# Moving weight loads, statistics, degrees and one scaling within the last attention batch of a graph-attention and aggregation kernel

## The chip, the cores and the metric

The kernel runs on one core of a Trainium2 chip. The metric is the device time of one execution in microseconds (us), as a median of several runs. A core has five engines with an instruction stream each: TensorE (PE) for matrix products, VectorE (DVE), ScalarE (ACT), GpSimd (POOL) and SyncE (SP); SP here does nothing but issue DMA transfers. The engines run side by side and wait for each other with semaphores. Within one engine the instructions run in the order in which they were written.

## The reference

Input `x` has 16 batches of 1024 nodes with 256 channels; `adj` is a 1024 x 1024 matrix. Layer 0, cut to what matters:

```python
g   = relu(einsum('bcn,bnm->bcm', x^T, adj * A_s) * para)   # A_s from the nodes' means
q   = g^T in 4 heads;  k, v = (x @ kv_w) in 4 heads
out = softmax(q k^T * scale) v
x1  = layernorm(x + out)
```

Layer 1 uses the same matrix, normalised by degrees:

```python
A_norm = A + eye(n)
deg    = A_norm.sum(0) + A_norm.sum(1) - diagonal(A_norm)
dinv   = rsqrt(deg)
agg    = einsum('nm,bmd->bnd', A_norm * dinv[:, None] * dinv[None, :], x1)
h      = relu(batchnorm(agg @ W1.T + b1))
y      = layernorm(x1 + batchnorm(h @ W2.T + b2))
```

The batch norms take their statistics over all batches and nodes, so layer 1 has stages that can't begin before the one ahead of them has gone through all batches.

## The kernel before

**Stages.** A first stage goes through the 16 batches and does layer 0 for each. It overlaps the preparation of batch b+1 (weights `wg`, products `p1` to `p7`) with the attention of batch b. A second stage aggregates and does the first linear layer, a third the second linear layer, a fourth the last norm and the output. The change lies in the last attention batch (b = 15), where there is no batch 16 to prepare; layer 1 is prepared in its place.

**Attention.** The work of one batch is 32 units `(b, pr, qh, m)`: a pair of heads, a half of the queries, and a block of 128 keys. `scores(i)` (L1058) has PE write a PSUM tile `ps` and ACT take its exponential into `p` (a pool of four buffers). `outputs(i)` (L1074) has PE add `p` times the values into two PSUM tiles `po`, and DVE add `p` into `acc`, the sums of the softmax. Eight units make a group with one `po` pair and one `acc`. At its end ACT copies one `po` into `oT`, DVE adds the other (L1105), transposes it into `oS` (L1115), and SP writes it out and gathers it back by rows. After both groups of a pair of heads, `normalise` (L1127) has PE sum `acc` over the partitions (`den`, L1134); the sums travel by way of DRAM into columns `dcol`, and `residual` (L1152) takes reciprocals on DVE (`r_all`) and has POOL scale and add (L1161, L1162).

**The order.** PE, ACT, DVE and SP follow the order in which the program issues. The units are taken two at a time, in 16 bursts u = 0 to 15 per batch. In a burst the program issues the scores of its two units, then `back(j - 1)`, the outputs of the two before, and then what hangs on the burst. For the last batch that is the table `last`, keyed by u; `before_last` is the same for batch 14. A place under 16 in the lists of `(function, places)` is a burst of batch 14, a place from 16 on is burst place - 16 of batch 15. Entries of one burst run in the order in which they were put into the table. So each line of these tables fixes where a piece of work stands in the queue of every engine that it uses.

**Preparation of layer 1.** For the transposed adjacency, SP loads it as squares of 32 x 32 (`load_adjacency_squares`, L1244: four transfers of 128 KB in pieces of 128 B, alternating between two single buffers, those of `xS` and `crow`); DVE transposes within the squares (`transpose_adjacency`, L1251); ACT sums a block's columns (`adjacency_columns`, L1255). `degrees` (L1260) has three small DVE instructions and a power on POOL. `row_of_degrees` (L1267) transposes the result on DVE and has SP write it to DRAM and read it back as a row on all partitions. `add_identity` (L1272) is on POOL, `scale_adjacency(m)` (L1277) on DVE. `load_weights` (L1199) loads W1 and W2, 512 KB each, and `transpose_weights` (L1206) turns them on PE and copies them on ACT. `load_x1l` (L1293) loads a batch of x1, 1 MB. `statistics_x1` (L1175) computes the layer norm's statistics of batch 14, two blocks per call, on DVE and ends in a chain of four small POOL instructions; `finish_x1` (L1180) applies it on ACT and stores x1.

**The end of attention.** After the last burst, `outputs` of the last unit issues `scale_adjacency(2)` and then the last `acc` addition (L1108 to L1110). Then `aggregate_first(m)` (L1299) runs the first batch's aggregation on PE for m = 0 to 7, with the scalings 3 to 7 issued at m = 0, the last `den` (`den_last`) after m = 1, and the sums `aT` for the next aggregations on DVE beside it. Each m needs its scaled block; the PSUM tiles of m = 0 are those that the last `po` held.

Of the kernel before, what the change touches and what calls it, by code (L numbers as in the profile page):

```python
# [515 lines left out]
def fast_path(  # L516
# [20 lines left out]
    B, N, C = x.shape  # L537
# [28 lines left out]
    def tile_o(name):  # L566
        return psum["o"].tile([P, HALF], F32, tag="o", name=name)
# [167 lines left out]
    with (  # L735
# [338 lines left out]
        def outputs(i):  # L1074
            b, pr, qh, m = units[i]
            s, p = st[b], A.pop(i)
            if m == 0:
                G[b, pr, qh] = {
                    "po": [tile_o(f"po_{i}_{kh}") for kh in range(2)],
                    "acc": accp.tile([P, N], F32, tag="acc", name=f"acc_{i}"),  # L1080
                }
            g = G[b, pr, qh]
            for hd in range(2):
                h = 2 * pr + hd
                for kh in range(2):
                    r = slice(kh * D, (kh + 1) * D)
                    nc.tensor.matmul(  # L1087
                        g["po"][kh][hd * D : (hd + 1) * D, :], s["v"][r, m, h * D : (h + 1) * D],
                        p[r, hd * HALF : (hd + 1) * HALF], start=(m == 0), stop=(m == NCH - 1),
                    )  # L1090
            def sums():
                if m == 0:
                    g["p0"] = p
                elif m == 1:
                    nc.vector.tensor_add(g["acc"], g.pop("p0"), p)
                else:
                    nc.vector.tensor_add(g["acc"], g["acc"], p)  # L1097

            if i < len(units) - 1:
                sums()  # L1100
            if m == NCH - 1:
                k = (b * PAIRS + pr) * 2 + qh
                g["oT"] = op.tile([P, HALF], F32, tag="oT", name=f"oT_{k}")
                nc.scalar.copy(g["oT"], g["po"][0])
                nc.vector.tensor_add(g["oT"], g["po"][1], g["oT"])  # L1105
                if (b, pr) != (B - 1, PAIRS - 1):
                    squares(b, pr, qh)
            if i == len(units) - 1:  # L1108
                scale_adjacency(2)
                sums()  # L1110

        def squares(b, pr, qh):
            k = (b * PAIRS + pr) * 2 + qh
            oS = osp.tile([P, HALF], F32, tag="oS", name=f"oS_{k}")
            nc.vector.transpose(oS, G[b, pr, qh]["oT"])  # L1115
            nc.sync.dma_start(o_d[k].rearrange("q i j d -> (q i) (j d)"), oS)
            rows_of.append((squares_to_rows, (b, pr, qh)))
# [159 lines left out]
        def scale_adjacency(m):  # L1277
            nc.vector.scalar_tensor_tensor(
                aht[m], aht[m], dinv[:, m : m + 1], aht["row"], op0=ALU.mult, op1=ALU.mult
            )  # L1280
# [43 lines left out]
        with tc.manual_schedule(  # L1324
# [27 lines left out]
            def back(j):  # L1352

                for i in bursts[j]:
                    outputs(i)
                b, pr, qh, m = units[bursts[j][-1]]
                if m == NCH - 1 and qh == 1:
                    sums.append((normalise, (b, pr)))
                    for q in range(2):
                        full.append((residual, (b, pr, q)))  # L1360
                    if pr == PAIRS - 1:
                        for f in (statistics_x1, finish_x1):
                            for ns in (range(NCH // 2), range(NCH // 2, NCH)):
                                late.append((f, (b, ns)))

            last, before_last = {}, {}
            for u, todo in (
                (1, (load_weights,)), (6, (load_x1l, 0)), (8, (degrees,)), (9, (row_of_degrees,)),
                (10, (transpose_weights, 0)), (11, (transpose_weights, 1)),
                (12, (add_identity,)), (13, (scale_adjacency, 0)), (14, (scale_adjacency, 1)),  # L1370
            ):
                last.setdefault(u, []).append((todo[0], todo[1:]))
            for f, places in (
                (transpose_adjacency, (9, 11, 13, 15, 17, 19, 21, 23)),
                (load_adjacency_squares, (6, 9, 9, 11, 13, 15, 17, 19)),
                (adjacency_columns, (11, 13, 14, 16, 18, 20, 22, 23)),
            ):
                for m, u in enumerate(places):
                    where = before_last if u < PERB else last
                    where.setdefault(u % PERB, []).append((f, (m,)))  # L1380
            for u, n in ((9, 6), (10, 7)):
                before_last.setdefault(u, []).append((adjacency_rows, (n,)))
            for i in range(4):
                ns = range(2 * i, 2 * i + 2)
                last.setdefault(6 + i, []).append((statistics_x1, (B - 2, ns)))
            for u, ns in ((13, range(2)), (14, range(2, 5)), (15, range(5, NCH))):
                last.setdefault(u, []).append((finish_x1, (B - 2, ns)))
            last[15].append((load_x1l, (1,)))
# [319 lines left out]
    with tc.tile_pool(name="hl", bufs=4) as hl, tc.tile_pool(name="o2p", bufs=1) as o2p:  # L1708
# [89 lines left out]
        for b in range(B):  # L1798
# [59 lines left out]
            for c in range(CC):  # L1858
                last = b == B - 1 and c == CC - 1
# [160 lines left out]
def kernel(tc: tile.TileContext, *args):  # L2020


    with tc.tile_pool(name="flag", bufs=1, space=DRAM) as flag:
        good_d = flag.tile([1, 1], I32, name="good_d")
        fast_path(tc, *args, good_d)
        good = tc.nc.values_load(good_d[0:1, 0:1], min_val=0, max_val=2 * P)
        with tc.If(good < 2 * P):
            general_path(tc, *args)
# [30 lines left out]
```

## Time and profile before

| what | value |
|---|---|
| median of 3 runs | 2470.86 us (2469.76 to 2471.12) |
| the profiled execution | 2469.28 us |
| its span, first to last instruction | 2467.5 us |
| PE busy | 2425.2 us |
| DVE busy | 1840.3 us |
| ACT busy | 1231.6 us |
| POOL busy | 479.9 us |

Stretches of the last attention batch, 20 us each, busy time in us:

| from, to | PE | DVE | ACT | POOL | DMA GB/s |
|---|---|---|---|---|---|
| 1500, 1520 | 20.00 | 16.69 | 15.44 | 4.19 | 96 |
| 1520, 1540 | 18.64 | 17.26 | 12.78 | 8.56 | 178 |
| 1540, 1560 | 18.66 | 14.17 | 12.71 | 7.03 | 61 |
| 1560, 1580 | 18.47 | 19.69 | 9.86 | 15.31 | 106 |
| 1580, 1600 | 20.00 | 19.46 | 0.93 | 8.77 | 1 |

Positions in time are us from the start of the span. Durations and spacings come from one profiled execution. A busy PE is a PE with matmuls in its pipeline: the next one begins before the one ahead has ended, so spacings of starts say more than sums of durations.

### The profile page before, as it was taken

To read this page: it belongs to the slowest core of one execution; us is meant where nothing else is said; L and a number is where in the kernel's file an instruction comes from. 1 tells how busy PE (TensorE), PEld (TensorE's weight loads), DVE (VectorE), ACT (ScalarE), POOL (GpSimd) and SP (SyncE) were. 2 spreads that over 40 slices of the span, in tenths; PEclk is the share of its full clock that TensorE was granted. 3 is DMA by queue.
4 is the path that set the end of the run, shared out by engine and by line. 5 is a ranking of instruction groups with operands and counts; after the bars stand their busy time and mean duration, and the time that the engine had idled before them with its cause. 6 is when DMAs were issued, how large, how long until landed. Compare 5 with 4: busy or idle time off the path is not lost.

```text
span 2467.5 us, 32796 instructions
## 1 busy us (share of the span) xinstructions
PE 2425.2 (98%) x12462; PEld 1035.2 (42%) x12462; DVE 1840.3 (75%) x2528; ACT 1231.6 (50%) x1535; POOL 479.9 (19%) x487
## 2 busy tenths in 40 slices
PE   8999999999999999999999999999999999999997
PEld 4343443443434434434434343344444444434455
DVE  5678878878888888788788888856555555578568
ACT  6375665765765766757657667311010010144458
POOL 0021112211211211121112113522112212000026
PEclk9999999999999999999999999999999999999999
DMA  3123232332232231323322327222122122255559
GB/s 136 31 48 84 54 53 69 69 51 67 39 82 60 41 86 54 52 69 69 53 68 47 72 52 116 54 101 102 69 86 102 68 85 102 91 200 175 182 190 340
DMA packets 414647, 220.42 MB, mean 89 GB/s; under 512 B 353168, under 2 KB 386448, under 8 KB 406032
## 3 DMA queue, kind: packets, MB, share of 16 engines
q1 hardware_dynamic: 409120, 167.36, 27.6%
q0 software_dynamic: 4832, 50.34, 4.9%
q8 instruction: 100, 1.64, 0.3%
q14 instruction: 67, 0.55, 0.1%
q10 hardware_dynamic: 528, 0.52, 0.1%
HBM read 134.49 MB, written 83.69 MB: 88 GB/s over the span
## 4 chain that ended last, share of the span: by engine, by line
PE 83%; DVE 10%; ACT 3%; DMA 2%; issue 1%; SPq 0%; POOL 0%; DVEq 0%; POOLq 0%
PE ps L1066 17%; PE po L1087 17%; PE pgb L896 7%; PE b_agg L1564 4%; PE pga L896 4%; PE c_agg L1564 4%; PE pk L993 3%; PE po L1846 3%; PE pv L1006 2%; PE a_agg L1564 2%; PE b_h L1596 2%; PE b_o L1772 2%; PE pgc L896 2%; PE pgd L896 2%; PE c_h L1596 2%; PE c_o L1772 1%
## 5 line engine op out<-in xcount | busy, mean ns | idle before, releaser
L1071 ACT ACTIVATE p<-ps 128x1024 f32<-128x1024 f32 x512 | 497.4, 1021 | 182.2 <-PE ps L1066 123.2
L1097 DVE TENSOR_TENSOR acc<-acc,p 128x1024 f32<-128x1024 f32 x384 | 501.4, 1306 | 52.3 <-ACT p L1071 28.9
L1066 PE MATMUL ps<-qT,kT 64*64 64x512 f32 x4096 | 488.3, 592 | 0.3 <-ACT p L1071 0.3
L1087 PE MATMUL po<-p,v 64*64 64x512 f32 x4096 | 485.6, 589 | 0.0
L1161 POOL TENSOR_TENSOR o<-o,r_all 128x512 f32<-128x512 f32 x62 | 95.9, 1555 | 1104.8 <-DVE r_all L1155 989.9
L1087 PEld LDWEIGHTS po<-p,v 64*64 64x64 f32 x4096 | 159.4, 133 | 280.1 <-issue 273.2
L1066 PEld LDWEIGHTS ps<-qT,kT 64*64 64x64 f32 x4096 | 152.4, 133 | 285.9 <-issue 248.5
L847 DVE SCALAR_TENSOR_TENSOR wg<-wg,adj_s 128x1024 f32<-128x1024 f32 x128 | 149.7, 1217 | 24.6 <-ACT wg L843 24.6
L838 ACT ACTIVATE wg<-crow,ccol 128x1024 f32<-128x1024 f32 x128 | 146.7, 1146 | 6.1 <-PE pg L978 6.1
L843 ACT ACTIVATE wg<-wg 128x1024 f32<-128x1024 f32 x128 | 135.9, 1062 | 0.9
L993 PE MATMUL pk<-xT,kvw_s 128*128 128x512 f32 x256 | 121.9, 598 | 3.1 <-ACT drow L1140 3.1
L1006 PE MATMUL pv<-kvw_s,xT 128*128 128x256 f32 x512 | 123.9, 385 | 0.0
L1006 PEld LDWEIGHTS pv<-kvw_s,xT 128*128 128x128 f32 x512 | 95.0, 190 | 50.3 <-issue 13.6
L906 ACT ACTIVATE qT<-qT 128x512 f32<-128x512 f32 x60 | 37.1, 626 | 149.8 <-DVE qT L909 145.3
L896 PE MATMUL pgb<-wg,S 128*128 128x512 f32 x240 | 111.0, 605 | 0.0
L896 PE MATMUL pga<-wg,x 128*128 128x512 f32 x240 | 109.6, 599 | 0.7 <-ACT qT L919 0.7
L1564 PE MATMUL a_agg<-ahT,x1l 128*128 128x512 f32 x240 | 108.1, 593 | 0.7 <-ACT agg L1312 0.7
L1564 PE MATMUL b_agg<-aT,x1S 128*128 128x512 f32 x240 | 107.9, 592 | 0.0
L1162 POOL TENSOR_TENSOR x<-x,o 128x512 f32<-128x512 f32 x62 | 106.9, 1734 | 2.4
L656 ACT COPY p_agg<-a_agg 128x512 f32<-128x512 f32 x15 | 8.8, 586 | 183.3 <-PE a_agg L1564 179.5
L1675 ACT ACTIVATE hl<-hl,bn_sh,bn_sg 128x1024 f32<-128x1024 f32 x64 | 75.6, 1232 | 40.7 <-DMA hl<-h 38.1
L692 POOL TENSOR_TENSOR x1S<-x1l 128x512 f32<-128x512 f32 x15 | 19.4, 1293 | 352.9 <-PE c_agg L1564 350.1
(234 smaller groups left out, 3495.8 us busy)
## 6 DMA issues: line engine op xcount, KB each, us to landing
h<-hw POOLq DMA_DIRECT2D x16, 2048.0 KB, 6.6
hl<-h SPq DMA_DIRECT2D x32, 1024.0 KB
x<-x POOLq DMA_DIRECT2D x16, 1024.0 KB, 4.3
x1l<-x SPq DMA_DIRECT2D x16, 1024.0 KB
xf<-x SPq DMA_DIRECT2D x16, 1024.0 KB
o<-oS SPq DMA_DIRECT2D x62, 256.0 KB
o<-o SPq DMA_DIRECT2D x248, 64.0 KB
x<-in_x_dram SPq DMA_DIRECT2D x15, 1024.0 KB
```

The costliest lines, as they stand in the source:

```text
L838: nc.scalar.activation(w, s["crow"], AF.Abs, bias=s["ccol"][:, n : n + 1])
L843: nc.scalar.activation(w, w, AF.Tanh, scale=0.5)
L847: nc.vector.scalar_tensor_tensor(w, w, 1.0, adj_s[:, n, :], op0=ALU.subtract, op1=ALU.mult)
L896: nc.tensor.matmul(ps, left, right, start=(start and i == 0), stop=(i == NCH // 2 - 1), skip_group_check=True,)
L993: nc.tensor.matmul(ps, kvw_s[:, c, kc * P : (kc + 1) * P], s["xT"][:, c, hs], start=(c == 0), stop=(c == CC - 1),)
L1006: nc.tensor.matmul(pt[:, j * C : (j + 1) * C], s["xT"][:, c, n * P : (n + 1) * P], kvw_s[:, c, C : 2 * C], start=(c == 0), stop=(c == CC - 1),
L1066: nc.tensor.matmul(ps[kh * D : (kh + 1) * D, hd * HALF : (hd + 1) * HALF], kT[r, pr, ks], qT[r, pr, qh * HALF : (qh + 1) * HALF], start=Tr ...
L1071: nc.scalar.activation(p, ps, AF.Exp)
L1087: nc.tensor.matmul(g["po"][kh][hd * D : (hd + 1) * D, :], s["v"][r, m, h * D : (h + 1) * D], p[r, hd * HALF : (hd + 1) * HALF], start=(m = ...
L1097: nc.vector.tensor_add(g["acc"], g["acc"], p)
L1162: nc.gpsimd.tensor_tensor(xs, xs, o, ALU.add)
L1564: nc.tensor.matmul(ps, left, right, start=(start and i == 0), stop=(i == NCH // 2 - 1), skip_group_check=True,)
```

## The change

Only places in the order change; no instruction is added, dropped or altered.

- `load_weights` goes from burst 1 of batch 15 to burst 7. It thereby stands on SP behind the loads of the adjacency's squares 6 and 7 and behind `load_x1l(0)`.
- The four calls of `statistics_x1` for batch 14 go from bursts 6 to 9 to bursts 8 to 11.
- `degrees`, `row_of_degrees`, both `transpose_weights`, `add_identity` and `scale_adjacency(0)` go one burst later each.
- The column sum of block 7 goes from burst 7 to burst 8.
- `scale_adjacency(1)` goes from burst 14 to the end of the last `outputs`, behind the last `oT` and ahead of scaling 2.

```diff
             if i == len(units) - 1:
-                scale_adjacency(2)
+                for k in (1, 2):
+                    scale_adjacency(k)
                 sums()
...
-                (1, (load_weights,)), (6, (load_x1l, 0)), (8, (degrees,)), (9, (row_of_degrees,)),
-                (10, (transpose_weights, 0)), (11, (transpose_weights, 1)),
-                (12, (add_identity,)), (13, (scale_adjacency, 0)), (14, (scale_adjacency, 1)),
+                (6, (load_x1l, 0)), (7, (load_weights,)), (9, (degrees,)), (10, (row_of_degrees,)),
+                (11, (transpose_weights, 0)), (12, (transpose_weights, 1)),
+                (13, (add_identity,)), (14, (scale_adjacency, 0)),
...
-                (adjacency_columns, (11, 13, 14, 16, 18, 20, 22, 23)),
+                (adjacency_columns, (11, 13, 14, 16, 18, 20, 22, 24)),
...
-                last.setdefault(6 + i, []).append((statistics_x1, (B - 2, ns)))
+                last.setdefault(8 + i, []).append((statistics_x1, (B - 2, ns)))
```

## The prediction

> **What bounds the kernel now.** I read the page first, then the waits of TensorE (PE), the stretches of the last attention batch, and the order of time on PE, VectorE (DVE), SyncE (SP) and GpSimd (POOL) there. PE carries the whole run:
>
> ```profile
> PE 2425.2 (98%) x12462; PEld 1035.2 (42%) x12462; DVE 1840.3 (75%) x2528; ACT 1231.6 (50%) x1535; POOL 479.9 (19%) x487
> ```
>
> So only time at which PE stands still can be won. The waits of PE before 1600 us hold two that lie in the region of the change:
>
> ```profile
> PE den L1134 <- DVE acc L1097: 2.7, 1, 2.7
> PE pagg L1305 <- DVE oT L1105: 1.5, 1, 1.5
> ```
>
> The first is the denominator product after the first pair of heads of batch 15; the second is the first aggregation, in a PSUM bank that the last `oT` addition must release. The order of time on PE prices both better than these waits do (columns: start, duration, engine, line, operation, count):
>
> ```profile
> 1507.06 1.90 PE L1087 MATMUL po<-p,v 64*64 64x512 f32 x16
> 1508.88 1.06 PE L1134 MATMUL den<-acc,ones 128*32 128x512 f32 x8
> 1509.88 1.95 PE L1066 MATMUL ps<-qT,kT 64*64 64x512 f32 x16
> ...
> 1535.68 1.98 PE L1087 MATMUL po<-p,v 64*64 64x512 f32 x16
> 1537.59 1.05 PE L1134 MATMUL den<-acc,ones 128*32 128x512 f32 x4
> 1541.34 1.05 PE L1134 MATMUL den<-acc,ones 128*32 128x512 f32 x4 [2.69 <-DVE acc L1097]
> 1542.32 1.95 PE L1066 MATMUL ps<-qT,kT 64*64 64x512 f32 x16
> ```
>
> Undisturbed, from the start of `po` to the next `ps` is 1509.88 - 1507.06 = 2.82 us; here it is 1542.32 - 1535.68 = 6.64. The stall costs 3.82, not 2.69: undisturbed, all eight rows of `den` take 1.00 together, and when torn apart each half takes as much. In the same way the first aggregation starts at 1570.60 and the `den_last` after its 16 rows at 1579.46, 8.86 later. Undisturbed, 24 rows take 1590.86 - 1580.45 = 10.41, so 16 take 6.94: this stall costs 1.92. Together 5.74 us.
>
> Why DVE is late is in its order of time:
>
> ```profile
> 1521.18 3.58 DVE L1097 TENSOR_TENSOR acc<-acc,p 128x1024 f32<-128x1024 f32 x2
> 1526.04 1.18 DVE L1095 TENSOR_TENSOR acc<-p,p 128x1024 f32<-128x1024 f32 x1
> 1529.37 1.25 DVE L1253 STREAM_TRANSPOSE ahT<-aS 128x1024 f32<-128x1024 f32 x1 [2.15 <-DMA aS<-in_adj_dram]
> 1530.54 2.51 DVE L1097 TENSOR_TENSOR acc<-acc,p 128x1024 f32<-128x1024 f32 x2
> 1532.97 0.42 DVE L620 BATCH_NORM_STATS2 st_l<-x 128x6 f32<-128x256 f32 x1
> ```
>
> It waits 2.15 us for adjacency square 6, then does four blocks of statistics before `acc` of the group is complete. The square's loads stand behind the weights on SP, and one issue of them took 3.58 us:
>
> ```profile
> 1518.24 0.63 SPq L1203 DMA_DIRECT2D wl<-in_L_gnn_W_dram  x1
> 1518.91 0.50 SPq L1204 DMA_DIRECT2D wl<-in_L_gnn_W_dram  x1
> 1520.57 3.58 SPq L1249 DMA_DIRECT2D aS<-in_adj_dram  x1
> ```
>
> **What the Trainium skill says.** "Perfetto Trace Analysis", section Identifying the Most-Contended Engine, says that matmul busy time measures nearness to the roofline badly, because matmuls are pipelined; hence I price stalls by starts, and the trace agrees (3.82 against a shown 2.69). "TensorEngine Tiling (Array Packing)", Key Properties, says that tiles of the array run independently; eight `den` rows in 1.00 us agree. "GPSIMD Engine Reference", Specifications, says that GpSimd shares its SBUF interfaces with VectorE, with contention when the latter has two SBUF inputs. The trace agrees: two `acc` additions beside `L1162` took 3.50 (1521.18 to 1524.68), alone 2.43 (1530.54 to 1532.97). "DMA: Bandwidth & Descriptors", Specifications, puts line rate at 512 B or more per transfer; the squares, in 128 B pieces, moved at 137 GB/s (1507 to 1510), a load of `x1l` in long rows at 401:
>
> ```profile
> 1507.00:1510.00 3.00, 3.00 (x32) 0.74 (x28) 1.66 (x3) 1.97 (x3) 0.00 (x0) 1.00 1.58 137
> 1538.00:1540.00 2.00, 0.64 (x4) 0.00 (x0) 1.83 (x6) 2.00 (x4) 1.01 (x1) 1.00 0.95 401
> ```
>
> **The change, part by part.** Nothing is added or dropped; instructions move. Prices, from start to start: `acc` 1.22 alone; a transposed square 1.17 (1498.36 to 1499.51 and others); statistics of two blocks 1.08 (1532.97 to 1534.05); `oT` and `oS` 0.7 each. I replay each engine in its new order.
>
> *Weights behind `x1l` 0 (burst 1 to 7).* SP reaches square 6 at 1518.24 instead of 1519.51, and 1 MB leaves the DMA ahead of it. Four issues take about 2.4 us, and the last piece of square 5 took 4.1 us to land (1505.97 to 1510.06): landing by about 1525, bounded by 1529.25 - 1.27 = 1528.0 if the missing megabyte helped nothing. DVE asks at 1527.15. I take no wait; the bound is 0.8. Square 7 still waits for DVE to release its buffer at 1521.25, lands near 1528, and is asked for at 1534. SP, free sooner, issues `oS` at 1526.1 instead of 1529.81, its four gathers by 1532, then `x1l` and both weights by 1534. Those 2 MB at 401 GB/s take 5 us: landed by about 1540, where PE wants them near 1549. Behind them on SP stand `oS`, the `den` rows (1539.6), `dcol`, four gathers, the degrees' row: `dcol` lands near 1545 for reciprocals at 1556, the row near 1552 for a scaling at 1561. Nothing shown, with 9 us of cover each.
>
> *Statistics (bursts 6-9 to 8-11).* Two pairs, 2 x 1.08 = 2.16 us, leave DVE ahead of `den`. DVE: square 6 at 1527.15; two `acc` from 1528.30, beside `L1162` on POOL until 1529.47, so 3.50; two more 2.44, to 1534.25; square 7 to 1535.4; the last two to 1537.85. PE wants `acc` at 1537.6, so about 0.3 us of wait stays (none if POOL doesn't slow DVE; 1.1 if square 6 is also late by its bound). First gain 3.82 - 0.3 = 3.5.
>
> *The column sum 7 (burst 7 to 8).* Before, ACT stood 3.59 us in front of it while the exponentials of the next burst waited behind. Now these go at 1535.1. The sum comes after `drow`, ends near 1540.6, and pushes the next two exponentials 0.7 us back, to 1540.55-1542.4; PE needs the score buffer at 1542.2 for one and 1543.1 for the other. Nothing.
>
> *Degrees, row, identity, weight transposes (each one burst later).* DVE after `den`: `oT`, `oS` to 1539.6; then per burst a pair of statistics and two `acc`, 1.08 + 2.44 = 3.5, plus 0.45 for the degrees and 0.15 for the row, against 3.44 of PE per burst and 4.46 where weights are transposed. It ends the statistics near 1550.5 and the group's `acc` near 1552.9; `oT` follows at 1554.5, and PE wants its bank at 1556.5. The second weight transposition now stands between `oT` and that use, which gives 1.0 more cover. GpSimd's chain for the statistics (5.4 us, 1546.58 to 1551.99) ends near 1555.9, and ACT asks for it at 1557.8.
>
> *Scalings.* Scaling 0 comes after two more `acc`, scaling 1 after the last `oT`. Before, scaling 1 took 2.29 us ahead of that `oT`. Now, beside POOL's `L1161` and `L1162` (8.5 us from 1556.6): two `acc` at 2.0 each to 1560.9, scaling 0 to 1563.1, three `acc` to 1567.7, `oT` 1567.8-1568.5. PE starts aggregating at 1570.60 - 3.5 - 0.2 = 1566.9 and wants that bank for its fourth product, 2.6 later, at 1569.5: covered by 1.0. Then three gates: scaling 1 by 1569.75, wanted 1570.35; scaling 2 by 1571.1 and the last `acc` by 1572.8, wanted 1573.85. Covered by 0.6 and 1.0 if these run as beside the weight sums of POOL (1.3); at the 1.8 of the five scalings after (9.09 for five), 0.1 us is left at the first gate and none is lost. I take 0.1 lost: second gain 1.8.
>
> **Sum.** 3.5 + 1.8 = 5.3 us. The later stages (aggregation, 36.4 us per batch) are paced by PE and pass it on; `aT` is ready near 1593.5 on DVE against PE's 1596.7. The profiled execution of 2469.28 (span 2467.5) becomes 2464.0; it lies 1.6 under the median shown, so the median becomes 2470.86 - 5.3 = 2465.5.
>
> **Rivals.** *The gates move (20%).* The waits shrink but stay: POOL's additions slow DVE more than taken, so `acc` comes at 1539 and the scalings at 2.2 each hold the aggregation. For it: those three instructions used to be done or half done by then. Against: 0.6 to 1.0 us of cover. Gain 3 to 4.9: 2466 to 2467.9, near 2466.8. *Nothing is won (4%).* The work only moves behind `den`; DVE falls behind by as much there, the four `p` buffers fill, exponentials and then PE wait. Against it: DVE stood idle 0.99 us ahead of 1552.58 and 4.18 ahead of 1559.32, room for the 4.3 us of statistics. 2470.9. *Slower (6%).* The statistics end late, GpSimd's chain with them, and ACT holds `finish_x1` with the last four exponentials queued behind. Place: ACT near 1557.8. It costs nothing until the statistics end 4 us after my 1550.5 (1.9 of cover on ACT, 2.1 on PE), then 1 us per us; the run is slower than before from 9.3 us late, which needs the additions of four bursts held up; by 15 us it is 2476.
>
> **How the numbers follow.** A difference of 0.2%, 4.94 us, is about what a measurement of this kernel can tell from no change. My 5.3 lies just past it. The forecast, 70%, is a gain of 4.9 to 5.9; the first rival and nothing won are "within", 23 to 24%; the rest is slower. Its own range is 2465.0 to 2466.0. The range to state begins at 2464.2 (the whole 5.74 and 0.9 for the spread of the runs shown, 2469.76 to 2471.12) and ends at 2468.4, which takes in the first rival.
>
> **What would show it.** Right: no wait of `ahT` for `aS` on DVE; `den` as one group of eight within 0.4 us of its `po`; from `po` to `ps` there about 3.1; `pagg` to `den_last` about 7; the weights on SP after `x1l`. Wrong: `den` still in two halves with over 1 us between, new waits of `pagg` on `ahT` scalings or of `den_last` on `acc`, or ACT idle ahead of `L630`.

## The result, and the profile after

| | before | after |
|---|---|---|
| median of 22 runs each, same chip | 2470.59 us (2469.49 to 2473.21) | 2466.84 us (2465.61 to 2467.71) |
| profiled execution, its span | 2469.28, 2467.5 | 2466.75, 2465.0 |

The kernel became faster by 3.75 us. The ratio is 0.9984, 95% interval 0.9977 to 0.9990: a real gain, but under the 0.2% that the forecast expected to pass. The forecast was 2465.5, a gain of 5.3.

From L1109 on, the line numbers of the kernel after are one higher than before. In it, TensorE has one wait left between 1500 and 1600 us; the two of the prediction are gone:

```profile
PE a_agg L1565 <- ACT agg L1313: 0.7, 1, 0.7
```

The order of time on TensorE in the kernel after, around the denominator product and at the first aggregation (start, duration, engine, line, operation, count):

```profile
1536.32 1.90 PE L1087 MATMUL po<-p,v 64*64 64x512 f32 x16
1538.15 1.73 PE L1135 MATMUL den<-acc,ones 128*32 128x512 f32 x8
1539.80 1.95 PE L1066 MATMUL ps<-qT,kT 64*64 64x512 f32 x16
...
1568.08 7.13 PE L1306 MATMUL pagg<-ahT,x1l 128*128 128x512 f32 x16
1575.15 1.07 PE L1135 MATMUL den_last<-acc,ones 128*32 128x512 f32 x8
...
1598.56 3.70 PE L1565 MATMUL a_agg<-ahT,x1l 128*128 128x512 f32 x8 [0.68 <-ACT agg L1313]
```

`den` is in one piece. In the program, its first four rows sum the `acc` of the first group and the other four that of the second, so only the second half depends on the late `acc`. The eight take 1.73 us here and 1.06 undisturbed, so a short wait is left inside the piece. From `po` to the next `ps` it is 1539.80 - 1536.32 = 3.48 us (profile of before: 6.64, undisturbed 2.82). From `pagg` to `den_last` it is 7.07 (8.86). From that `po` to `a_agg`, the first matmul behind all of this, it is 62.24 (67.19). So the first profiles show a local gain of 4.95 us; the clocked gain is 3.75.

VectorE and SyncE (queue) in the kernel after, where VectorE used to wait for square 6:

```profile
1526.51 1.27 DVE L1095 TENSOR_TENSOR acc<-p,p 128x1024 f32<-128x1024 f32 x1
1527.70 1.23 DVE L1254 STREAM_TRANSPOSE ahT<-aS 128x1024 f32<-128x1024 f32 x1
1528.87 6.31 DVE L1097 TENSOR_TENSOR acc<-acc,p 128x1024 f32<-128x1024 f32 x4
1535.09 1.24 DVE L1254 STREAM_TRANSPOSE ahT<-aS 128x1024 f32<-128x1024 f32 x1
1536.25 2.51 DVE L1097 TENSOR_TENSOR acc<-acc,p 128x1024 f32<-128x1024 f32 x2
```

```profile
1518.77 6.08 SPq L1250 DMA_DIRECT2D aS<-in_adj_dram  x8
...
1532.96 0.57 SPq L1296 DMA_DIRECT2D x1l<-x  x1
1533.58 0.43 SPq L1204 DMA_DIRECT2D wl<-in_L_gnn_W_dram  x1
```

The weights stand behind `x1l`, the transposition of square 6 follows without a wait, and no statistics stand ahead of `acc`. It is complete at 1536.25 + 2.51 = 1538.76, a little after TensorE began with `den`.

### The profile page after: what moved, and what is told of

Same layout as the page of the kernel before. It is cut to its first block, busy times and chain, and to the rows that moved or that the text cites. A ratio compares the mean times of both kernels' runs of the same rounds, so it can differ in the third digit from the quotient of the medians.

```text
span 2465.0 us, 32797 instructions
## 1 busy us (share of the span) xinstructions
PE 2427.8 (98%) x12462; PEld 1036.2 (42%) x12462; DVE 1840.8 (75%) x2528; ACT 1231.0 (50%) x1535; POOL 475.5 (19%) x487
## 4 chain that ended last, share of the span: by engine, by line
PE 86%; DVE 9%; ACT 3%; DMA 1%; issue 1%; POOL 0%; POOLq 0%; DVEq 0%
PE ps L1066 18%; PE po L1087 18%; PE pgb L896 7%; PE b_agg L1565 4%; PE pga L896 4%; PE c_agg L1565 4%; PE pk L993 4%; PE po L1847 3%; PE pv L1006 2%; PE a_agg L1565 2%; PE b_h L1597 2%; PE b_o L1773 2%; PE pgc L896 2%; PE pgd L896 2%; PE c_h L1597 2%; PE c_o L1773 1%
## 5 line engine op out<-in xcount | busy, mean ns | idle before, releaser
L1162 POOL TENSOR_TENSOR o<-o,r_all 128x512 f32<-128x512 f32 x62 | 94.8, 1537 | 1097.8 <-DVE r_all L1156 1059.5
L1163 POOL TENSOR_TENSOR x<-x,o 128x512 f32<-128x512 f32 x62 | 106.9, 1734 | 2.4
```

Of the source, the lines that this page charges most:

```text
L1163: nc.gpsimd.tensor_tensor(xs, xs, o, ALU.add)
```

## The experiments

Spacings are those above: D, from the `po` ahead of the torn `den` to the next `ps`; G, from the first `pagg` to `den_last`; and L, from that `po` to `a_agg`. All are us. The ratio is to the kernel before in the same comparison; it and its interval are the comparison's own, not the quotient of two medians.

| kernel | median | ratio, 95% interval | D | G | L |
|---|---|---|---|---|---|
| before, first profile | 2470.59 | | 6.64 | 8.86 | 67.19 |
| before, second and third profile | 2470.70, 2470.59 (one run each) | | 5.40, 5.41 | 8.85, 8.86 | 65.95, 65.95 |
| after | 2466.84 | 0.9984 [0.9977, 0.9990] | 3.48 | 7.07 | 62.24 |
| after, second profile | 2467.23 | 0.9982 [0.9975, 0.9989] | 3.48 | 7.06 | 62.24 |
| weights alone | 2471.32 | 0.9998 [0.9989, 1.0007] | 5.39 | 8.86 | 65.94 |
| statistics alone | 2468.47 | 0.9988 [0.9981, 0.9995] | 3.57 | 8.86 | 64.13 |
| scaling 1 alone | 2470.22 | 0.9998 [0.9989, 1.0007] | 7.54 | 8.14 | 67.87 |
| weight transposes alone | 2468.89 | 0.9989 [0.9980, 0.9997] | 5.40 | 7.23 | 64.32 |
| all but scaling 1 | 2467.32 | 0.9984 [0.9977, 0.9991] | 3.48 | 7.39 | 62.56 |
| all but the weights | 2467.85 | 0.9982 [0.9975, 0.9988] | 4.38 | 7.06 | 63.14 |
| after, square 7 later | 2467.14 | 0.9982 [0.9974, 0.9989] | 2.82 | 7.07 | 62.65 |
| after, square 7, its sums and degrees later | 2465.52 | 0.9976 [0.9966, 0.9986] | 2.87 | 7.07 | 61.63 |

The medians of the kernel before in the four comparisons were 2470.59 (for the kernel after), 2471.25 (weights, statistics and scaling 1 alone, all but scaling 1), 2471.64 (transposes alone, square 7 later, after's second profile) and 2471.66 (all but the weights, the last row).

### The kernel before, profiled again

> The kernel before once more, as a look at its granted clock. Theory: its first profile lay low because no dip fell in it; this one shows dips of the clock to 0.6-0.9 for 4-8 us after the boundaries at about 2184 or 2380 us, and a span of 2468.5-2470.5. Rival: the dips belong to the kernels with the change; this profile has none and a span of 2467-2468. The local spacings repeat in either case (po to ps 6.6, first pagg to den_last 8.9, po to a_agg 67.2).

> The kernel before, a third look, for the landing of square 6. Theory: VectorE's wait for it is either 0.6-0.9 us, with po to ps 5.3-5.5, or 2.1-2.3 us, with po to ps 6.5-6.7, and nothing between; the clock dips after 2180 or 2376 us. Rival: the waits spread evenly, and po to ps takes any value.

VectorE in the second profile of before, at square 6:

```profile
1526.85 1.21 DVE L1095 TENSOR_TENSOR acc<-p,p 128x1024 f32<-128x1024 f32 x1
1528.88 1.25 DVE L1253 STREAM_TRANSPOSE ahT<-aS 128x1024 f32<-128x1024 f32 x1 [0.82 <-DMA aS<-in_adj_dram]
1530.05 2.67 DVE L1097 TENSOR_TENSOR acc<-acc,p 128x1024 f32<-128x1024 f32 x2
```

GpSimd there:

```profile
1529.04 1.28 POOL L1162 TENSOR_TENSOR x<-x,o 128x512 f32<-128x512 f32 x1
```

The wait for the square is 0.82 us, in the third profile 0.79; in the profile that the forecast was worked out from it was 2.15. So the 6.6 that was expected again did not come; the dips of the clock did (last section). A fairer measure is the time from the start of that `acc` to the start of the transposition, since a longer addition hides part of a wait. In the seven profiles with the weights ahead of the squares it is 1.81, 1.95, 2.02 and 2.03 us in four, and 2.93, 3.33 and 3.40 in three, the first profile of before among the latter. So the square lands early or late by about 1.2 us, from execution to execution, and the den stall of the kernel before is 2.58 us (D 5.40) in the one case and 3.82 (6.64) in the other. One of the square's four loads takes long to issue, 3.45 to 3.80 us in the three late profiles and 2.98 to 3.32 in the four early ones; that goes with a late landing, but is too small to be all of it, and what makes a landing late was not tried.

From a profile of before with an early landing to the kernel after, L falls by 65.95 - 62.24 = 3.71 us. The second profiles on both sides also agree to the end: the first `ph` of the next stage, at 2150.22 before and 2146.39 after, is 3.83 earlier, and the spans, 2468.9 and 2465.4, differ by 3.5. The medians differ by 3.75 in the first comparison and by 4.41 (2471.64 - 2467.23) in the third.

### The weights alone

```diff
-                (1, (load_weights,)), (6, (load_x1l, 0)), (8, (degrees,)), (9, (row_of_degrees,)),
+                (6, (load_x1l, 0)), (7, (load_weights,)), (8, (degrees,)), (9, (row_of_degrees,)),
```

> The kernel before with one edit: the weights' loads go from burst 1 to burst 7. Mine: VectorE's wait for square 6 (2.15 us) goes and the column of waits shows none of ahT for aS; from the start of po to the next ps at the torn den falls from 6.64 to about 4.5 us (6.64 - 2.15, or 5.5 if the two acc additions now stand beside GpSimd's addition, +1.06); from the first pagg to den_last stays near 8.9. Time 1 to 2 us shorter. Rival, the statistics alone made acc late: 6.6 stays.

VectorE with the weights alone moved:

```profile
1526.37 1.25 DVE L1095 TENSOR_TENSOR acc<-p,p 128x1024 f32<-128x1024 f32 x1
1527.54 1.23 DVE L1253 STREAM_TRANSPOSE ahT<-aS 128x1024 f32<-128x1024 f32 x1
1528.71 3.58 DVE L1097 TENSOR_TENSOR acc<-acc,p 128x1024 f32<-128x1024 f32 x2
```

and GpSimd there:

```profile
1528.60 1.27 POOL L1162 TENSOR_TENSOR x<-x,o 128x512 f32<-128x512 f32 x1
```

The wait for the square is gone and D is 5.39, the same as before with an early landing. No difference in time shows, though the interval is wide enough to hold a gain of 1.25 us. From the start of L1095 to the end of the two `acc` it is 1532.29 - 1526.37 = 5.92 us here and 1532.72 - 1526.85 = 5.87 in the second profile of before. The additions now run while GpSimd's L1162 does, and two take 3.58 us instead of 2.67: what the wait gave back, they lost. The loss follows the overlap. With 0, 0.27, 0.29, 0.41 and 1.16 us of L1162 still to run when the first of the two begins (before's three profiles, the run with the transposes alone, and this one), they take 2.51, 2.67, 2.71, 2.83 and 3.58. Only against a late landing does the edit win, 6.64 - 5.39 = 1.25.

### The statistics alone

```diff
-                last.setdefault(6 + i, []).append((statistics_x1, (B - 2, ns)))
+                last.setdefault(8 + i, []).append((statistics_x1, (B - 2, ns)))
```

> The kernel before with one edit: the four calls of the statistics go from bursts 6-9 to 8-11. Mine: the wait of 2.15 us for square 6 stays, two pairs of statistics (2.16 us) leave VectorE ahead of den, so po to ps falls from 6.64 to about 4.5; first pagg to den_last stays near 8.9. Time about 2 us shorter. Rival, the square's wait alone: 6.6 stays.

TensorE with the statistics alone moved:

```profile
1537.17 1.97 PE L1087 MATMUL po<-p,v 64*64 64x512 f32 x16
1539.08 1.73 PE L1134 MATMUL den<-acc,ones 128*32 128x512 f32 x8
1540.74 1.95 PE L1066 MATMUL ps<-qT,kT 64*64 64x512 f32 x16
```

`den` is whole, and D is 3.57. This profile had an early landing (a wait of 0.63), so it compares with 5.40: the statistics win 1.83 of the 1.92 us between before and after (5.40 - 3.48). They are the first gain where the square lands early; where it lands late, the weights add to it (1.25 above without the statistics moved, 0.90 with them, below).

### Scaling 1 alone, and all without it

The first kernel is before with this; the second is after with the opposite.

```diff
             if i == len(units) - 1:
-                scale_adjacency(2)
+                for k in (1, 2):
+                    scale_adjacency(k)
                 sums()
...
-                (12, (add_identity,)), (13, (scale_adjacency, 0)), (14, (scale_adjacency, 1)),
+                (12, (add_identity,)), (13, (scale_adjacency, 0)),
```

> The kernel before with one edit: scaling 1 goes from burst 14 to behind the last oT. Mine: po to ps at den stays 6.64; first pagg to den_last falls from 8.86 to about 7.0 to 7.1, with no wait of pagg for oT. Time about 1.8 us shorter. Rival, the gates move: pagg then waits for ahT or den_last for acc, and the spacing stays over 8.

> The changed kernel with one part undone: scaling 1 stays in burst 14. Mine: po to ps at den about 3.5 as in the changed kernel; first pagg to den_last near 8.9 as before the change, because scaling 1 again stands ahead of the last oT. Time about 3.2 us shorter than before. Rival, the second stall went because the work ahead of it came earlier, not because of the scaling: near 7.1, and 5 us shorter.

With scaling 1 alone moved, the aggregation waits at the next gate in place of the bank:

```profile
1572.45 3.83 PE L1305 MATMUL pagg<-ahT,x1l 128*128 128x512 f32 x8
1576.99 3.24 PE L1305 MATMUL pagg<-ahT,x1l 128*128 128x512 f32 x7 [0.72 <-DVE ahT L1278]
```

G falls by 0.72 only, to 8.14. With all the rest of the change and scaling 1 in its old place G is 7.39, so on top of the rest the move is worth 7.39 - 7.07 = 0.32. It isn't where the second gain comes from, though without it 0.45 of a stall is left (6.94 undisturbed).

### The weight transposes alone

```diff
-                (10, (transpose_weights, 0)), (11, (transpose_weights, 1)),
+                (11, (transpose_weights, 0)), (12, (transpose_weights, 1)),
```

> The kernel before, with nothing changed but the two halves of the weight transposition one burst later (11 and 12 instead of 10 and 11). Theory, formed on the runs so far: the second gain (first pagg to den_last 8.86 -> 7.07) comes from this. The second half then lies on TensorE between the end of the third group of po, which releases VectorE's and GpSimd's work, and the last group, so that work starts about 1.2 us earlier against TensorE. First pagg to den_last falls from 8.86 to 7.2-7.6; the den stall stays whole (po to ps 6.4-6.9); po to a_agg falls from 67.2 by 1.3-1.7 us; the time falls by 0.5 to 1.7 us, the rest of which is lost in the noise of the end. Rival: it is worth nothing, and the second gain was won by the earlier den (VectorE no longer behind): first pagg to den_last stays at 8.7-8.9 and po to a_agg at 67.

TensorE in this kernel, from the end of the third group on:

```profile
1554.64 1.90 PE L1087 MATMUL po<-p,v 64*64 64x512 f32 x16
1556.47 1.09 PE L1224 MATMUL pw<-ident,wl 128*128 128x128 f32 x8
1557.49 1.95 PE L1066 MATMUL ps<-qT,kT 64*64 64x512 f32 x16
...
1569.67 7.30 PE L1305 MATMUL pagg<-ahT,x1l 128*128 128x512 f32 x16
```

For comparison, the kernel before there:

```profile
1553.96 1.09 PE L1224 MATMUL pw<-ident,wl 128*128 128x128 f32 x8
...
1556.76 1.90 PE L1087 MATMUL po<-p,v 64*64 64x512 f32 x16
```

GpSimd's scaling and the last `oT`, in the kernel before:

```profile
1561.34 4.02 POOL L1161 TENSOR_TENSOR o<-o,r_all 128x512 f32<-128x512 f32 x2 [9.35 <-DVE r_all L1155]
...
1574.24 0.68 DVE L1105 TENSOR_TENSOR oT<-po,oT 128x512 f32<-128x512 f32 x1
```

and with the transposes alone moved:

```profile
1559.23 4.02 POOL L1161 TENSOR_TENSOR o<-o,r_all 128x512 f32<-128x512 f32 x2 [7.13 <-DVE r_all L1155]
...
1571.68 0.68 DVE L1105 TENSOR_TENSOR oT<-po,oT 128x512 f32<-128x512 f32 x1
```

G falls to 7.23, so this one move wins 1.63 of the 1.79 us. L falls by the same 1.63 (65.95 to 64.32), while D stays at 5.40. The second `pw` stood ahead of the `po` that ends the third group; now it stands behind. That `po` releases `oT`, and behind it in VectorE's order come the reciprocals, which release GpSimd's L1161 and L1162; beside these VectorE is slow (two `acc` from 1562.39 took 4.05 us before, against 2.51 alone). TensorE's 1.02 us of `pw` (1556.47 to 1557.49) are then spent while that work runs instead of ahead of it. L1161 starts 1570.60 - 1561.34 = 9.26 us ahead of `pagg` before, and 1569.67 - 1559.23 = 10.44 here; in the kernel after it is 10.44 too. The last `oT` ends 4.32 after the first `pagg` before and 2.69 after it here, where the bank is wanted at about 2.6. Of these 1.63 us, 1.18 are the earlier start; the other 0.45 are the three additions ahead of the last `oT`, which took 5.74 before and 5.29 here. A quicker release plays no part: `oT` of the third group starts 2.56 after its `po` before (1559.32 - 1556.76) and 2.57 after it here (1557.21 - 1554.64).

### All but the weights

```diff
-                (6, (load_x1l, 0)), (7, (load_weights,)), (9, (degrees,)), (10, (row_of_degrees,)),
+                (6, (load_x1l, 0)), (1, (load_weights,)), (9, (degrees,)), (10, (row_of_degrees,)),
```

> The kernel after with only the loads of the weights back in burst 1, ahead of the squares 6 and 7. Theory: their landing in front of the squares comes in two sizes (VectorE waits 0.6-0.8 us or 2.15-2.2 us for square 6), and in the first case the wait is worth nothing, as the additions lose the same time beside GpSimd when they come earlier: po to ps 3.4-3.7 and po to a_agg 62.2-62.5 with a wait of 0.6-0.8; po to ps 4.0-4.9 with a wait of 2.2. The median is 0 to 1 us above after's. Rival: the weights are half of the first gain, as the forecast had them: po to ps 4.5 or more even with the short wait.

TensorE and VectorE in this kernel:

```profile
1537.21 2.03 PE L1087 MATMUL po<-p,v 64*64 64x512 f32 x16
1539.17 1.05 PE L1135 MATMUL den<-acc,ones 128*32 128x512 f32 x4
1540.61 1.05 PE L1135 MATMUL den<-acc,ones 128*32 128x512 f32 x4 [0.38 <-DVE acc L1097]
```

```profile
1527.62 2.06 DVE L1095 TENSOR_TENSOR acc<-p,p 128x1024 f32<-128x1024 f32 x1
1530.55 1.25 DVE L1254 STREAM_TRANSPOSE ahT<-aS 128x1024 f32<-128x1024 f32 x1 [0.88 <-DMA aS<-in_adj_dram]
```

By the wait alone (0.88) this would count as an early landing, for which 3.4 to 3.7 was expected, and D is 4.38: both sentences of the expectation missed. L1095 took 2.06 here, so the square came 2.93 after its start: a late landing with a part of its wait hidden. For that case 4.0 to 4.9 was given. In this one profile `den` is torn again, for a wait of 0.38, and the weights' place is worth 4.38 - 3.48 = 0.90. With an early landing and the statistics moved it is 0.09 (3.57 against 3.48, from the run with the statistics alone).

### Square 7 and its sums a burst later, and the kernel after again

The first kernel is the kernel after with the first of these edits, the second has all of them.

```diff
-                (transpose_adjacency, (9, 11, 13, 15, 17, 19, 21, 23)),
+                (transpose_adjacency, (9, 11, 13, 15, 17, 19, 21, 24)),
...
-                (6, (load_x1l, 0)), (7, (load_weights,)), (9, (degrees,)), (10, (row_of_degrees,)),
+                (6, (load_x1l, 0)), (7, (load_weights,)), (10, (degrees,)), (11, (row_of_degrees,)),
...
-                (adjacency_columns, (11, 13, 14, 16, 18, 20, 22, 24)),
+                (adjacency_columns, (11, 13, 14, 16, 18, 20, 22, 25)),
```

> The kernel after, with the last of the adjacency squares transposed one burst later (burst 8 of the last batch instead of 7), so that VectorE's two transposes of 1.24 us do not stand ahead of the additions that the torn den of burst 8 waits for. Theory: VectorE then ends acc about 1.2 us earlier, the 0.66 us left over of the first stall goes: po to ps 3.48 -> 2.8-2.9, po to a_agg 62.24 -> 61.6, and the time is 0.3-0.7 us below that of the kernel after in the same comparison. Rival: the transpose only meets another deadline one burst later (oT of the second group, or the columns that ScalarE writes), po to ps falls to 2.9 but po to a_agg stays at 62.2 and the time is that of the kernel after.

> The kernel after once more, beside the others. Theory that the granted clock's dips after the stage boundaries (2180 us and 2376 us) come by chance and not by the change: this profile has them at some boundary or at none, at other depths than the first, and the local spacings repeat (po to ps 3.5, first pagg to den_last 7.1, po to a_agg 62.2). Rival, that the change brings them: the same dips at 2180 and 2376 us, and none in the kernel before beside it.

> The kernel after, with square 7 transposed in burst 8 (as before), its column sums in burst 9 instead of 8, and degrees and their row in bursts 10 and 11, one later each, since they need the sums. In the run that moved the square alone, TensorE won 0.66 at den and lost 0.79 at the next scores, since ScalarE's column sums, ahead of two exponentials, waited 1.59 us for the transposition. Theory: with the sums a burst later the loss goes: po to ps 2.8, no wait of ps for p behind it, po to a_agg 61.4-61.8 (after: 62.24), and a median 0.3-0.8 us below after's, which is about the size that the comparison can just not tell. Rival: the degrees' row then comes too late for the first scaling (the row's issue moves from 1549.7 to about 1553 us, the first scaling is at 1561.7), and the first aggregation waits: first pagg to den_last over 7.5, or po to pagg above 32.2, and nothing is won.

With the square alone, TensorE waits for an exponential that stands behind the column sums on ScalarE:

```profile
1542.98 2.00 PE L1066 MATMUL ps<-qT,kT 64*64 64x512 f32 x16 [0.79 <-ACT p L1071]
```

```profile
1540.87 1.06 ACT L1257 ACTIVATE ahT<-ahT 128x1024 f32<-128x1024 f32 x1 [1.59 <-DVE ahT L1254]
```

The 0.66 us left of the first stall go (D 2.82), but L rises from 62.24 to 62.65, and the time is that of the kernel after. With the sums a burst later too, the wait is gone and L is 61.63, 0.61 less than after. The median of 2465.52 is 6.14 below before and 1.71 below the kernel after in its second comparison. Its interval and that one's overlap, and of the 1.71 only 0.61 is a shorter order of work; this profile also had no dip of the clock (below). It is the fastest kernel run here.

The kernel after repeated its spacings to 0.01 us, and its dips of the clock at 2180 and 2376 us. So the dips did not come elsewhere or at other depths, as its theory had it, but the rival falls too: the second and third profile of before have theirs at the matching places. Besides the first profile of before, three show no dip there: those with scaling 1 alone, with the transposes alone, and this last one.

## Why the prediction was right and wrong

The time lies inside the range (2464.2 to 2468.4), 1.3 us above the predicted one. The sign was right; the outcome held likeliest, a gain of 4.9 to 5.9, did not come, and the range holds the time because it took in the first rival. Of the gain, 1.55 us are missing (5.3 - 3.75).

- **Right: the place and the kind of the gain.** Both waits went; `den` came in one group, no `ahT` waits for `aS`, the weights went behind `x1l`, and TensorE waits for nothing new. Late statistics, the late degrees' row and the late column sum cost nothing in the trace.
- **Wrong: "The stall costs 3.82" as the base of the first gain.** That was one execution with a late landing of square 6. The two other profiles of the kernel before have 2.58. The forecast carried the difference of the profiled time to the median (1.6 us) over, but not the chance that the wait itself isn't the usual one. This is 1.24 of what is missing, if the executions behind the medians mostly landed early.
- **Mis-sized: the leftover, "about 0.3".** It is 3.48 - 2.82 = 0.66. That is 0.36 of what is missing. Most of it, 0.28, lies in the four `acc` from square 6 to square 7: they took 1535.09 - 1528.87 = 6.22, where 3.50 + 2.44 = 5.94 was put. They also ran beside GpSimd's addition of the identity (L1276, at 1531.94), which the replay does not name. In the run with the weights back, L1163 was over before the four began, and they took 1536.88 - 1531.72 = 5.16 where 4 x 1.22 = 4.88, again 0.28 more, with L1276 beside them; that it is the cause was not tried apart. With both terms, 5.3 - 1.24 - 0.36 = 3.70, against 3.71 in the spacings from an early landing. That 3.75 was clocked is partly luck: from a late landing the spacings give 4.95, three landings of seven were late, and the third comparison clocked 4.41. How the landings divide over the runs behind the medians is not known.
- **Right sum, wrong cause: the second gain.** 1.8 was forecast and 1.79 came. It was put down to scaling 1 leaving its place ahead of the last `oT`; that move is worth 0.72 alone and 0.32 on top of the rest. The weight transposition behind the end of the third group is worth 1.63 alone. The forecast named it as "1.0 more cover" and gave it no gain, though its times contain it: they move the third group's `oT` by 4.8 us (1559.3 to 1554.5) and TensorE by 3.7 (1570.6 to 1566.9). Scaling 1 was priced too high: its 2.29, added to the replay's last `oT`, would end that 1.3 us past the bank's time (1568.5 + 2.29 - 1569.5). With scaling 1 in its old place and all the rest moved it ended 2.84 after `pagg`, 0.2 past the 2.6 at which the bank is wanted. So that the sum came out is luck.
- **Of the weights.** "I take no wait" was right. But the time freed is worth next to nothing (0.01 and 0.09 in D) where the square lands early, because the additions meet GpSimd's instruction. The forecast priced that collision in the sum of both moves and not as what cancels this one.
- **The rivals.** The time fell where the first one put it (2466 to 2467.9), and `acc` came later than forecast, as that rival had it. Its second half did not happen: no scaling holds the aggregation in the kernel after. Neither "nothing is won" nor the late chain of the statistics showed.

## What to carry to other kernels

Before a stall is priced from one profile, look at the same wait in two or three more: the one on a DMA here had two sizes, and each profile showed only one. Where work of the busiest engine must be done somewhere, try it behind the instruction that releases the others' next work, so that it runs while they catch up; here that was worth 1.63 us. And a wait that is taken away on an engine is worth only what the instructions behind it don't lose by starting beside a neighbour.

## What the runs showed of the hardware

The granted clock of TensorE drops for a few us after a short idle of it, in some executions and not in others, at the same place. Here is a stretch after a stage boundary, of the kernel before in its first profile (columns: stretch, its length, busy time of PE, weight load, DVE, ACT and POOL with counts, granted clock, DMA share, GB/s):

```profile
2184.00:2188.00 4.00, 3.52 (x9) 1.28 (x8) 3.72 (x6) 0.41 (x1) 0.00 (x0) 1.00 0.02 4
```

and in its second profile:

```profile
2184.00:2188.00 4.00, 3.94 (x6) 1.61 (x6) 3.40 (x6) 0.00 (x0) 0.00 (x0) 0.60 0.01 4
```

TensorE stood idle for 2.42 us ahead of both; in the first profile:

```profile
2183.36 1.10 PE L1772 MATMUL b_o<-o,w2S 128*128 128x512 f32 x2 [2.42 <-issue]
```

In one the clock stays at 1.00, in the other it is 0.60. A second dip follows at about 2380 us. From `ph` to the end of the span the second profile takes 1.7 us longer than the first (it is 0.33 ahead at `ph` and 1.4 behind at the end). Nine of the thirteen profiles have a dip at the first of these places, kernels of both sorts among them, so it isn't the change that brings it. The two first profiles differ by only 2.5 us in span, with a local gain of 4.95, for two reasons. The `po` from which L is counted came 0.64 later in the kernel after (1536.32 against 1535.68), as it did in the second profile of before (1536.60); and behind `ph`, where after is 4.40 ahead (2150.55 - 2146.15), it loses 1.9, with two dips that the first profile of before has not. The Trainium skill, "TensorE: Matmul & The Clock Gate", Part 1, says that a monitor lowers the clock after an idle window of about 3.4 us, and that the window runs freely, so that the moment of a change varies from run to run. The come and go between executions fits that; the idle here, 2.42 us, is shorter than such a window, so the page alone does not explain the drop. What decides it was not tried.

The den stall may bring a dip too; one run shows it. In the run with scaling 1 alone moved, the second half of the torn `den` took 1.92 us after its wait, and the stretch from 1540 to 1544 us had a clock of 0.66:

```profile
1541.84 1.92 PE L1134 MATMUL den<-acc,ones 128*32 128x512 f32 x4 [2.77 <-DVE acc L1097]
```

With a wait of 2.69 in the first profile of before it took 1.05. So D of 7.54 in that run is the late landing's 6.64 and 0.9 of a slow clock.

A group of matmuls that is torn by a wait costs more than the wait that the profile shows: 3.82 us for 2.69, 2.58 for 1.54, and 1.56 (4.38 - 2.82) for 0.38, so 1.04 to 1.18 more each time. The reason can be read from the lines: a half of `den` takes about 1.0, as long as the whole undisturbed.
